# How the first pass of a Fourier-layer kernel stores its chunks: 120 and 8 partitions with 8 KB rows in place of 128 and 128 with 4 KB rows

## The chip, the cores and the metric

The kernel runs on one core of a Trainium2 chip. The metric is the time on the device, in microseconds (us), of one execution; smaller is better. The core has a tensor engine (PE, with its weight loads PEld), a vector engine (DVE), a scalar engine (ACT), GpSimd (POOL) and a sync engine (SP) that here only issues transfers. Sixteen DMA engines carry every transfer between the on-chip memory (SBUF, 128 partitions) and the device memory (HBM).

## What is computed

The reference turns 64 images of 256 x 256 into tokens and runs one transformer layer on them. The front part is a Fourier neural operator of four layers on 32 channels, and it is what the change touches:

```
v = concat([x, gx, gy]) @ p_w + p_b                  # 64 x 32 x 256 x 256
for i in range(4):
    x1 = irfft2(12 x 12 low modes of rfft2(v), mixed over channels by fw1[i], fw2[i])
    x2 = einsum('bcxy,cd->bdxy', v, w_w[i]) + w_b[i]
    v = x1 + x2
    v = (v - mean) * rsqrt(var + eps) * bn_g[i] + bn_b[i]   # mean, var over b, x, y
    if i < 3: v = relu(v)
out = einsum('bcxy,cu->bxyu', v, q_w) + q_b
```

Behind it come a concatenation with 77 text rows, an attention over 333 tokens and a feed-forward block on half of the tokens. All is float32.

## The kernel before, in words

The mean and variance of a layer need all images, so the kernel makes passes. `forward_first` (L215) takes the input's low modes, and `mix` (L428) turns modes into mixed modes and the statistics, once for each of the four layers. Between them stand three passes of `layer` (L546, i = 0, 1, 2), which make the new `v` of layer i and at once what the next layer needs of it. A last stage (`image_rows` L960, `attention` L1054, `feed_forward` L1121) makes the output. `v` is 64 x 8 MB of float32, 512 MB, so it goes through HBM: pass 0 writes it, passes 1 and 2 read the old and write the new, the last stage reads it.

In HBM `v` is one tensor for an image, `[128, 8, 8, S]` (L183): partition, chunk t, row of the chunk, y. A chunk (b, t) is one eighth of an image, 1 MB: 8 rows of 256 numbers on each of 128 partitions, 8 KB a partition that lie together both in SBUF and in HBM; the partitions of one chunk lie 64 KB apart in HBM.

For each chunk `layer` does:

- `pre` (L676): matmuls into four PSUM banks, held as two pairs, from `y_` (the x transform of the mixed modes) and, in pass 0, from `mv` (the y table with four rows of the input x, reloaded for each image by `load_x`, L637, from POOL's queue). In passes 1 and 2 the old `v` comes in instead, through `ld` (L652). `pre` also takes a new `vo` buffer from the pool `lo`, which has 4 (L561, L698).
- `evA` and `evB` (L700): the ReLU of one bank pair into one half of `vo`: evA fills rows 0 to 3, evB rows 4 to 7, each on ACT (L705) or DVE (L707) as the order says.
- `st` (L711): stores `vo` to HBM with two transfers from SP's queue.
- `turn` (L716, DVE transpose L719), `prod` (L724, L730) and `sqA`, `sqB` (L736, L741: squares on ACT for the next statistics) read `vo` too. `y`, `zt`, `half`, `x`, `xo` and `xs` (L745 to L803) make the next layer's modes of an image.

A `vo` buffer is free for the fifth chunk after it when its stores have landed and `turn` and `prod` have read it. PSUM is a ring of four pairs handed out by `take` (L602): a `pre` or a `prod` needs two, and gets those that were closed first.

The order of all this is written out by hand in `ORDER` (L128), one word a step, the first string for pass 0. A suffix `.a` or `.d` names ACT or DVE, `@1` means that the step works on the next image. `layer` runs under a manual schedule, so each engine and each queue takes its instructions in this order. In pass 0 the chunks come in the order 2, 3, 6, 4, 5, 7, 1, 0 (the last two an image ahead), so that chunk 7 takes the buffer of chunk 3, 5 that of 2, 1 that of 6, 0 that of 4, and 2, 3, 6, 4 those of 5, 7, 1, 0 of the image before. SP's queue has, for each image: st1, st2, st0, the two loads of `ams` (mixed modes, L623), st6, st3, st5, st4, st7 and the store `xs`. Chunk 3 is thus stored behind chunk 6.

```
    def st_(b, t, e):
        for n in range(2):
            rows = slice(4 * n, 4 * n + 4)
            nc.sync.dma_start(dst[b][:, t, rows], vo[b, t][:, rows])
```

Of the kernel before, what the change touches and what calls it, by code (L numbers as in the profile page):

```python
# [153 lines left out]
def tile_fno_fusion_transformer(ctx: ExitStack, tc: tile.TileContext, a, cst_d, grid_d, out):  # L154
    nc = tc.nc
# [390 lines left out]
    def layer(i, st, src, dst, acc):  # L546
# [7 lines left out]
        with ExitStack() as cx:  # L554
# [64 lines left out]
            y_, t32, vin, vo, half_, zts = {}, {}, {}, {}, {}, {}  # L619
# [89 lines left out]
                return run  # L709

            def st_(b, t, e):  # L711
                for n in range(2):
                    rows = slice(4 * n, 4 * n + 4)
                    nc.sync.dma_start(dst[b][:, t, rows], vo[b, t][:, rows])
# [87 lines left out]
            def xs(b, n, e):  # L802
                nc.sync.dma_start(xh_d[i][:, b, :], xos.pop(b).rearrange("p g k -> p (g k)"))  # L803

            run = dict(
                am=am, lx=lx, ld=ld, sp=sp, spT=spT, pre=pre, evA=ev(0), evB=ev(1), st=st_, turn=turn,
                prod=prod, sqA=sq(0), sqB=sq(1), y=y, half=half, zt0=zt(0), zt1=zt(1), x=x_, xo=xo, xs=xs,
            )
# [425 lines left out]
```

## Time and profile before

| what | value |
|---|---|
| median of 3 runs | 11274.17 us (11272.87 to 11285.87) |
| the profiled execution's own time | 11293.58 us |
| its span, first to last instruction | 11291.7 us |
| PE, DVE, ACT, POOL busy | 94%, 75%, 57%, 13% of the span |
| DMA packets, bytes | 972,544; 3457.29 MB |
| `v<-vo` (L714), all three passes | 3072 transfers of 512 KB, median 7.8 us from issue to landing |
| the same in pass 0, 300 to 2400 us | least 2.6, median 4.9, most 10.0 us |
| `vin<-v` (L656), passes 1 and 2 | 2048 transfers of 512 KB, 9.1 us |
| `ch<-v` (L980), last stage | 512 transfers of 1024 KB, 12.5 us |

The stages in the span, from the trace: 0 to 200 us the first modes, the first `mix` and the tables; 200 to 2525 pass 0; 2525 to 2667 `mix`; 2667 to 5480 pass 1; 5480 to 5640 `mix`; 5640 to 8500 pass 2; 8500 to 8700 the last `mix` and the weights; from 8700 the transformer.

How to read what follows. Lnnn is a line of the kernel. In a list of waits each line has the engine and line that waited, behind the arrow what ended the wait, then the total in us, the number of times and the longest. In a chain each line has a start, a duration and what was at work, all in us. In a table of stretches each line has the stretch, its length, the busy time of PE, PEld, DVE, ACT and POOL with the number of instructions in brackets, the clock that PE was granted, the mean busy share of the 16 DMA engines and the GB/s that they moved. SPq is SP's queue of issues. The trace also holds a record of every DMA packet with its queue, start, duration and size, but not its engine. It tells when a transfer landed for about a quarter of the stores. Where a busy PE is told, note that matmuls are pipelined and their ends modelled, so waits of less than a microsecond can lie inside busy time.

### The profile page before, as it was taken

The page shows a single profiled execution, that of the slowest core. Times are in us where ns is not written, and L with a number is a line of the kernel's source. Part 1 is how long each engine was busy: PE and PEld are TensorE (multiplying, and loading weights), DVE is VectorE, ACT ScalarE, POOL GpSimd, SP SyncE. Part 2 cuts the span into 40 slices and gives each one's busy share as a digit, 9 for nine tenths or more (in the row PEclk, how much of TensorE's full clock was granted, in tenths as well). Part 3 has the DMA queues.
Part 4 walks back from the last instruction along what each step waited for, and adds up shares of the span by engine and source line. Part 5 has one row for each costly group of instructions (what it writes and reads, how often), then busy time and mean ns, then how long its engine had stood idle before and what let it go on. Part 6 is the DMA issues. An engine that isn't in the chain of part 4 may idle for free.

```text
span 11291.7 us, 409300 instructions
## 1 busy us (share of the span) xinstructions
PE 10625.0 (94%) x182550; PEld 5738.0 (51%) x182550; DVE 8446.5 (75%) x10381; ACT 6473.1 (57%) x10673; POOL 1442.4 (13%) x2179
## 2 busy tenths in 40 slices
PE   6999999998999999999799999999996999999999
PEld 3555555554444444444444444444443666666666
DVE  6888888887777777777677777777775666666665
ACT  5777777775566655566555566655563333333333
POOL 1111111110000000000000000000000333333333
PEclk8999999998999999999899999999998999999999
DMA  6776676678999999999899999999998555555553
GB/s 213 247 250 244 249 247 248 246 253 320 383 376 382 380 377 372 374 379 379 305 375 380 380 376 378 381 380 376 372 379 291 226 227 228 227 227 228 226 227 140
DMA packets 972544, 3457.29 MB, mean 306 GB/s; under 512 B 149784, under 2 KB 199320, under 8 KB 903832
## 3 DMA queue, kind: packets, MB, share of 16 engines
q1 hardware_dynamic: 905344, 3366.80, 77.8%
q0 software_dynamic: 58288, 60.60, 2.3%
q8 instruction: 1428, 23.40, 0.8%
q10 hardware_dynamic: 7144, 3.72, 0.1%
q14 instruction: 340, 2.79, 0.1%
HBM read 1733.60 MB, written 1696.92 MB: 304 GB/s over the span
## 4 chain that ended last, share of the span: by engine, by line
PE 62%; DMA 20%; DVE 9%; ACT 3%; issue 3%; SPq 2%; POOL 0%; ACTq 0%; DVEq 0%; POOLq 0%
PE ring L752 15%; DMA v<-vo 11%; PE ring L682 9%; PE ring L730 8%; DMA vin<-v 6%; PE ring L693 5%; PE hp L982 4%; PE ring L662 3%; PE pp L1145 3%; PE pp L1156 3%; PE ring L786 2%; DVE vo L707 2%; PE pp L1110 2%; PE pp L1175 2%; PE pp L1072 1%
## 5 line engine op out<-in xcount | busy, mean ns | idle before, releaser
L741 ACT ACTIVATE ring<-ring 128x1024 f32<-128x1024 f32 x3072 | 3115.8, 1014 | 1188.4 <-PE ring L730 1119.5
L719 DVE STREAM_TRANSPOSE t<-vo 128x2048 f32<-128x2048 f32 x1536 | 3465.7, 2286 | 20.9 <-DVE vo L707 0.9
L730 PE MATMUL ring<-vo,w 32*32 32x512 f32 x49152 | 2413.1, 600 | 85.0 <-ACT vo L705 68.3
L707 DVE TENSOR_SCALAR vo<-ring 128x1024 f32<-128x1024 f32 x1280 | 1544.5, 1221 | 1199.7 <-PE ring L693 806.6
L705 ACT ACTIVATE vo<-ring 128x1024 f32<-128x1024 f32 x1792 | 1791.7, 1023 | 1044.1 <-PE ring L693 500.9
L752 PE MATMUL ring<-t,cst 32*32 32x512 f32 x49152 | 2072.0, 599 | 51.0 <-issue 44.9
L752 PEld LDWEIGHTS ring<-t,cst 32*32 32x32 f32 x49152 | 913.4, 103 | 925.6 <-issue 622.6
L730 PEld LDWEIGHTS ring<-vo,w 32*32 32x32 f32 x49152 | 803.2, 103 | 1070.2 <-issue 407.1
L693 PE MATMUL ring<-vin,ws 32*32 32x512 f32 x32768 | 1287.8, 603 | 22.9 <-issue 16.2
L682 PE MATMUL ring<-cst,y 24*128 24x256 f32 x16384 | 1230.3, 402 | 77.0 <-DVE vo L707 61.7
L682 PEld LDWEIGHTS ring<-cst,y 24*128 24x128 f32 x16384 | 789.5, 185 | 993.2 <-DVE vo L707 392.4
L631 POOL TENSOR_TENSOR ams<-ams,bns 48x512 f32<-48x512 f32 x384 | 400.5, 1043 | 6989.4 <-DMA ams<-mix 6510.1
L670 DVE STREAM_TRANSPOSE y<-ring 128x1024 f32<-128x1024 f32 x384 | 763.1, 1987 | 329.5 <-PE ring L662 328.5
L682 PE MATMUL ring<-mv,y 29*128 29x256 f32 x8192 | 705.3, 403 | 36.3 <-ACT ring L741 19.6
L682 PEld LDWEIGHTS ring<-mv,y 29*128 29x128 f32 x8192 | 456.9, 185 | 369.0 <-ACT ring L741 209.3
L786 PEld LDWEIGHTS ring<-cst,zt 128*128 128x128 f32 x4608 | 533.6, 193 | 177.1 <-ACT vo L705 114.2
L762 ACT COPY half<-ring 128x1024 f32<-128x1024 f32 x192 | 194.4, 1013 | 731.4 <-PE ring L752 731.4
L1183 POOL DMA_DIRECT2D out_dram<-o x1024 | 508.2, 505 | 659.0 <-DVE o L1178 616.9
L741 ACT ACTIVATION_READ_ACCUMULATOR ring<-ring 128x1 f32 x3072 | 585.6, 191 | 0.0
L786 PE MATMUL ring<-cst,zt 128*128 128x96 f32 x4608 | 565.6, 280 | 6.1 <-DVE zt L770 5.7
L770 DVE STREAM_TRANSPOSE zt<-ring 128x1024 f32<-128x1024 f32 x192 | 377.4, 1965 | 248.1 <-PE ring L752 248.1
L662 PE MATMUL ring<-ams,cst 49*128 49x512 f32 (+1 forms) x1536 | 450.6, 642 | 99.1 <-POOL ams L631 37.2
(374 smaller groups left out, 9762.6 us busy)
## 6 DMA issues: line engine op xcount, KB each, us to landing
v<-vo SPq DMA_DIRECT2D x3072, 512.0 KB, 7.8
vin<-v SPq DMA_DIRECT2D x2048, 512.0 KB, 9.1
ch<-v SPq DMA_DIRECT2D x512, 1024.0 KB, 12.5
mix<-ob SPq DMA_DIRECT2D x96, 512.0 KB, 5.6
ams<-mix SPq DMA_DIRECT2D x384, 96.0 KB, 8.0
xin<-in_x_dram SPq DMA_DIRECT2D x16, 1024.0 KB, 6.5
mv<-in_x_dram POOLq DMA_DIRECT2D x256, 64.0 KB, 7.4
out_dram<-o POOLq DMA_DIRECT2D x1024, 16.0 KB, 3.0
```

Of the source, the lines that this page charges most:

```text
L662: nc.tensor.matmul(ps[:, n, :], lhsT=EX[hv, 128 * h:128 * h + 128], rhs=ams[b % 2][hv], start=True, stop=True, skip_group_check=True,)
L670: nc.vector.transpose(y_[b, h].rearrange("p q c -> p c q"), ring[key][0][1].rearrange("p n (c k) -> p (n c) k", k=32),)
L682: nc.tensor.matmul(ps[n][:, 256 * r:256 * r + 256], lhsT=y_[b, t // 4][32 * n:32 * n + K, q:q + 4, :].rearrange("p q c -> p (q c)"), rhs=m ...
L693: nc.tensor.matmul(ps[n][32 * j:32 * j + 32], lhsT=ws[32 * n:32 * n + 32], rhs=v[32 * n:32 * n + 32, 2 * j:2 * j + 2, :], start=False, sto ...
L705: nc.scalar.activation(to, ring[key][h][1], AF.Relu)
L707: nc.vector.tensor_scalar(to, ring[key][h][1], 0.0, None, ALU.max)
L719: nc.vector.transpose(t32[b, t // 2][:, :, 8 * (t % 2):8 * (t % 2) + 8, :].rearrange("p y s c -> p s y c"), vo[b, t].rearrange("p s (y l) ...
L730: nc.tensor.matmul(ps[n][32 * j:32 * j + 32], lhsT=w4[i + 1][32 * n:32 * n + 32], rhs=vo[b, t][32 * n:32 * n + 32, 2 * j:2 * j + 2, :], st ...
L741: nc.scalar.activation(ps, ps, AF.Square, accum_out=acc[:, at:at + 1])
L752: nc.tensor.matmul(ps[n][32 * j:32 * j + 32], lhsT=FYT[32 * n:32 * n + 32, k, :], rhs=t32[b, j][32 * n:32 * n + 32, k].rearrange("p s c -> ...
L786: nc.tensor.matmul(ps[:, 0, 96 * g:96 * g + 96], lhsT=zt_[:, h, k0:k0 + 4, :].rearrange("p k c -> p (k c)"), rhs=FX[:, h, 48 * r:48 * r + ...
L1183: nc.gpsimd.dma_start(out[b, 64 * n + 16 * g:64 * n + 16 * g + 16].rearrange("(p t) d -> p t d", t=2), o[32 * g + 8 * n:32 * g + 8 * n + 8 ...
```

## The change

In pass 0 (`i == 0`) a chunk is stored by two transfers that split the partitions rather than the rows: partitions 0 to 119 with their whole 8 KB, and partitions 120 to 127 with theirs. The bytes, their places in HBM, the queue, the number of transfers and their place in the order are the same. The first of the two transfers now reads both halves of `vo`. Passes 1 and 2 keep the two transfers of 128 partitions with four rows each.

```diff
             def st_(b, t, e):
+                if i == 0:
+                    for part in (slice(0, 120), slice(120, 128)):
+                        nc.sync.dma_start(dst[b][part, t], vo[b, t][part])
+                    return
                 for n in range(2):
                     rows = slice(4 * n, 4 * n + 4)
                     nc.sync.dma_start(dst[b][:, t, rows], vo[b, t][:, rows])
```

## The prediction, made before the changed kernel was run

> **What bounds the kernel now.** I read the slices of the page first, then the busy times by stage, then the waits inside the first pass, then its chain.
>
> ```profile
> PE   6999999998999999999799999999996999999999
> ...
> DMA  6776676678999999999899999999998555555553
> ```
>
> The digits are tenths of a slice of 282 us. PE is at nine tenths nearly everywhere; the DMA engines are at six or seven tenths in the first pass (slices 2 to 9) and full in the next two. The stages in figures (the last two columns are the DMA share and GB/s):
>
> ```profile
> 200.00:2525.00 2325.00, 2257.05 (x42675) 1181.56 (x42654) 2065.57 (x1148) 1774.20 (x2807) 270.83 (x380) 1.00 0.70 248
> ...
> 2562.90:2564.90 2.00, 1.13 (x71) 1.13 (x74) 1.38 (x5) 1.91 (x3) 0.00 (x0) 1.00 0.73 154
> ...
> 3000.00:3100.00 100.00, 94.65 (x2083) 43.69 (x2087) 76.00 (x42) 58.60 (x94) 6.27 (x6) 1.00 0.99 385
> ```
>
> The first pass lasts 2325 us for 64 images, 36.4 us each, with DMA at 0.70. The two other lines are for later use: with all partitions at work a full DMA carries 385 GB/s, and while `mix` stores 64 partitions (L495) 0.73 of it carries only 154, or 211 when full. The waits from 300 to 2400 us (total, times, longest):
>
> ```profile
> PEld ring L730 <- ACT vo L705: 155.6, 288, 2.1
> ...
> ACT vo L705 <- DMA v<-vo: 26.4, 41, 1.9
> ...
> DVE vo L707 <- DMA v<-vo: 5.1, 7, 0.9
> ```
>
> So the stores do end waits, about once an image, but only 31.5 us in 2100, or 35 us in the whole pass. Where, the chain of one image shows:
>
> ```profile
> 1594.22 1.03 ACT vo L705
> ...
> 1595.70 0.38 SPq L714
> 1596.08 0.05 issue
> 1596.14 0.78 SPq L714
> 1596.91 0.05 issue
> 1596.97 10.13 DMA v<-vo
> ...
> 1607.20 1.03 ACT vo L705
> 1608.23 0.04 issue
> 1608.28 2.06 PE ring L730 x32
> 1610.33 1.73 PE ring L786 x14
> ```
>
> An eviction ends (chunk 6, evA6), SP issues the stores of chunks 6 and 3 together, the last needs 10.13 us to land, and only then may chunk 7 be evicted into chunk 3's buffer; `prod` (L730) and `x` (L786) follow. I matched the instructions with the order written at L128: over 45 images st6 was issued 0.36 and 0.84 us after evA6, st3 1.68 and 3.10 us after it, and the second half of st3 landed at 10.97 (medians). It landed a median of 0.41 us before ev7 began, in the tightest of the 13 images that tell 0.07. For the other buffers this slack is 3.25 us (chunk 4 to chunk 0; least 2.0) or 6.7 and more. One edge is tight, and PE hangs on it at once.
>
> [...] The trace before shows only the 16: an st6 after idle time starts 16 packets within 0.16 us. [...] `mix`'s 64 partitions [...]: its 4 KB packets take 0.32 us, twice 0.16. And the final stage's 16 KB stores of eight partitions (L1183): a 2 KB packet alone takes 0.084 us, eight together 0.08 to 0.21, all done 0.32 us after the first began[...].
>
> **The change part by part.** All of it is in L711 to L714, run 512 times; nothing moves in SP's queue, and there are two issues a chunk as before (0.38 us median).
>
> *Rows of 8 KB.* 65,536 packets fewer. The final stage's 8 KB packets take 0.313 us, twice 4 KB 0.32: under 0.1 us a chunk gained. I count nothing.
>
> *The first store waits for both evictions.* Behind it on SP is only the second store, which waited for the same eviction before; nobody later in the queue is delayed. What is lost is the head start of one half, up to the time between the evictions (st6 is issued at 0.36 and 0.84, so 0.4 us). In the burst of st6 and st3 the engines are full, so the start counts, not the halves: between 0 and 0.4 us; I take 0.1.
>
> *The 120 rows.* [...] 8 x 0.313 = 2.5 us, against 16 x 0.16 = 2.56 before. [...] No run here shows how 120 rows are dealt out. Bounds -0.06 and +2.5 us; I take -0.06 and leave the rest to a rival.
>
> *The 8 rows.* [...] 4 x 0.313 = 1.25 us; at least 0.31 if the engines come one after another. The L1183 stores show the sharing, so I take 1.25.
>
> [...] 2.5 + 1.25 = 3.75 us a chunk against 2.56, +1.2. Share of the pass: 8 x 3.75 = 30 us an image, and other traffic 2.9 us (0.70 less the 0.62 of these stores, of 36.4): 33 of 36.4 us, tight but not over. On the path: st6 and st3 are two chunks in a burst, so st3 lands 2 x 1.2 + 0.1 = 2.5 us later; less the slack of 0.41, ev7 starts 2.1 us later. PE's next work waits for it (L730 behind ACT L705 above), and DVE and ACT behind PE, so I see no cover. The edge from 4 to 0 has st5 and st4 in one burst, +2.4 us against a slack of 3.25 that grows by the delay of ev7: it holds, though fuller queues (the `ams` loads, the `mv` loads of L638[...]) can add 0 to 0.5 us; I take 0.2. Sum: 2.3 us x 64 images = 147 us. [...]
>
> Durations are of the profiled execution: 11,293.6 us, of which the span is 11,291.7 and 1.9 lie around it; this is 0.17% over the median 11,274.2 of the runs. I add the sum to the median: **11,421 us**. Its own range is 11,350 to 11,520: 64 x 1.2 us if the eight rows are half spread, 64 x 3.8 if both edges bind.
>
> **The rivals.**
> *Pairs [...] (slower, more).* For it: `mix`'s packets double [...]. [...] Half in step, a row costs 0.47 us: 8 x 0.47 + 1.25 = 5.0 us a chunk, 40 us an image, with the rest 43, and about one more that the queue can't fill: 44 - 36.4 = 7.6 us, x 64 = 486, **11,760 us**. DMA becomes the bound of the pass. In step throughout: 8 x 6.25 + 2.9 = 53 us an image, 12,340, which I hold for unlikely[...].
> *The stores stay hidden (no change).* The eight rows go out while the engines of the 120 are staggered[...]. Then a burst of two chunks costs 2 x (2.5 + 0.31 - 2.56) = 0.5 us, about the slack of 0.41: 64 x 0.1 = 6 us, **11,280 us**.
> *Faster.* The mechanism: in the burst behind evA6, st3 shares engines with three `mv` loads (L638)[...] and some 4 KB packets there take 1.2 us. [...] its tail shortens by up to 0.6 us. It decides as soon as that exceeds what the eight rows add, at evB7 (L707/L705). The wait it can remove is 35 us in all: **11,240 us**. Against it: pre7 ends only about 0.1 to 0.3 us before ev7 starts, so there is no more to win.
>
> **How the numbers follow.** Chances: forecast 0.38, pairs 0.27, no change 0.21, faster 0.14. About 0.2% (23 us) is what a measurement of this kernel can tell from none. Slower by more: all of the first two and 0.03 of the third, 0.68. Faster by more: 0.10 of the last. Within: 0.22. The range runs from 11,250 (leaving out 0.06 of the faster case) to 11,830 (leaving out about 0.09, the pairs mostly in step).
>
> **What would show it.** In the changed kernel's first pass: ACT's wait for `v<-vo` at the eviction line up from 26 us to some 150; images 38.7 us apart instead of 36.4; DMA packets about 907,000; 8 KB packets of 0.31 us in the large store, and of about 1.2 in the small one. 8 KB packets of 0.6 us throughout, with GB/s in slices 2 to 9 near 200, mean pairs. [...] The other stages must keep their lengths (2813, 2860 and 2591 us). I am wrong if 120 and 8 rows are dealt to all 16 engines by partition[...].

## The result, and the profile after

The changed kernel takes 11,491.3 us (median of 4 runs, 11,479.0 to 11,492.2) beside 11,280.0 for the kernel before (4 runs): ratio 1.0187, 95% interval 1.0175 to 1.0199. That is 211 us more, where 147 were forecast. The profiled execution has a span of 11,489.6 us, 197.9 over the one before. The issue of the last store of the first pass ends at 2724.1 us instead of 2522.5: the pass alone is 201.6 us longer, and the stages behind it keep their lengths.

The slices of the page after the change, PE and DMA in tenths and what the DMA moved in GB/s, then the count of packets:

```profile
PE   6999999997999999999989999999997999999999
...
DMA  6777777777999999999989999999998655555553
GB/s 206 220 228 236 228 226 229 229 231 238 381 384 379 383 376 374 381 381 377 361 325 380 375 381 379 376 375 381 371 375 309 232 231 231 222 221 222 229 230 144
DMA packets 902396, 3457.24 MB, mean 301 GB/s; under 512 B 145176, under 2 KB 194712, under 8 KB 768152
```

PE is again at nine tenths in the first pass, and the DMA engines at seven: busier than before (there sixes and sevens), for fewer bytes a second, yet not full. One stretch of the pass, 300 to 2500 us, in the kernel before and in the changed one (stretch, length, PE, PEld, DVE, ACT, POOL, clock, DMA share, GB/s):

```profile
300.00:2500.00 2200.00, 2138.87 (x40500) 1123.37 (x40498) 1955.52 (x1089) 1678.68 (x2659) 257.60 (x361) 1.00 0.70 248
```

```profile
300.00:2500.00 2200.00, 2021.31 (x37474) 1029.08 (x37473) 1811.65 (x1005) 1555.38 (x2458) 237.18 (x331) 0.98 0.76 229
```

In the same time PE did 37,474 matmuls instead of 40,500. It was busy for 118 us less, and its granted clock fell from 1.00 to 0.98. The waits in this stretch, changed kernel:

```profile
PEld ring L734 <- ACT vo L705: 201.5, 250, 2.9
PEld ring L756 <- issue: 197.8, 389, 5.1
...
PE ring L756 <- issue: 63.7, 38, 4.2
...
ACT vo L705 <- DMA v<-vo: 57.0, 53, 2.3
...
PEld ring L682 <- issue: 48.5, 41, 4.3
...
DVE vo L707 <- DMA v<-vo: 31.6, 34, 2.1
...
PE ring L682 <- issue: 19.9, 12, 3.9
```

The evictions wait for stores for 88.6 us (57.0 + 31.6; 33.3 before). But there is a second group: waits of PE and of its weight loads that end with `issue`, that is, with nothing that the profile shows. Before, the same three lines read:

```profile
PEld ring L752 <- issue: 116.2, 430, 1.6
...
PEld ring L682 <- issue: 5.1, 7, 0.8
PE ring L752 <- issue: 2.1, 6, 0.7
```

(L752 then is L756 now.) The wait of the matmuls themselves at this line went from 2.1 us to 63.7, and its longest from 0.7 to 4.2 us. On the chain of waits such a stop stands beside a late store (parts of one image, left-out lines marked):

```profile
1553.13 1.23 ACT ring L745 x3
1554.36 2.61 issue
1556.97 1.20 PE ring L682 x16
...
1567.91 1.95 ACT vo L705 x2
...
1570.63 1.06 SPq L714
1571.70 0.04 issue
1571.74 9.74 DMA v<-vo
```

**What ends these stops.** The page has a queue named instruction, q8, with the same line in this kernel and in the one before (packets, MB, share of the engines):

```profile
q8 instruction: 1428, 23.40, 0.8%
```

That is 16 KB a packet, and 64 bytes for each of PE's 365,100 matmuls and weight loads (23.40 MB over 365,100): I read it as the fetch of PE's program. In the first pass one comes about every 7 us (318 from 300 to 2500 us before, 294 after). I call a stretch of over 1 us in which neither a matmul nor a weight load runs a stop, and a *fetch stop* if it ends 1.1 to 1.8 us after the end of a q8 packet (chance would give one in ten). From 300 to 2500 us the kernel before has none; the changed one has 55 stops, 99.2 us, of which 36 are fetch stops, 74.5 us. The fetches themselves are not slower (median 949 ns, before 967): they start late.

That PE lacked instructions can be checked without the times. 16 KB are 256 instructions of 64 bytes. If PE's 365,769 records (365,100 and the sequencer's) are numbered in order, all 36 fetch stops lie behind a record with the same remainder modulo 256, namely 193. Of the other 19 stops one does. So PE stops where a block ends. The same count gives how many records PE had left when each fetch started: in none of the 14 traces more than 303, thus little more than one block. Fewer than 60 were left in 11 of 318 fetches before (never under 34), and in 61 of 294 in the changed kernel, 23 of them with none.

The clock is slower too: it stood at 0.5 for 68.3 us in 16 pieces (before: never), and 13 of the 16 begin from 0.5 us ahead of the end of a stop of 1.5 us or more to 2 us behind it. At half speed 68.3 us lose 34.

So an image takes 39.55 us on average instead of 36.46 (images 4 to 63). In the 2200 us, PE and its loads idle together for 3.19 us an image instead of 0.99, which is +2.20, of which the fetch stops are 1.34 (74.5 us over 55.6 images); the slow clock is 34 us over as many, +0.61; 0.28 of the 3.09 us remain unassigned.

### The profile page after: what moved, and what is told of

Its sections match the earlier page's. It is cut to its first block, busy times and chain, and to the rows that moved or that the text cites. A ratio compares the mean times of both kernels' runs of the same rounds, so it can differ in the third digit from the quotient of the medians.

```text
span 11489.6 us, 408919 instructions
## 1 busy us (share of the span) xinstructions
PE 10677.8 (93%) x182550; PEld 5732.2 (50%) x182550; DVE 8451.8 (74%) x10381; ACT 6472.9 (56%) x10673; POOL 1442.2 (13%) x2179
## 2 busy tenths in 40 slices
DMA packets 902396, 3457.24 MB, mean 301 GB/s; under 512 B 145176, under 2 KB 194712, under 8 KB 768152
## 3 DMA queue, kind: packets, MB, share of 16 engines
q8 instruction: 1428, 23.40, 0.8%
## 4 chain that ended last, share of the span: by engine, by line
PE 52%; DMA 20%; DVE 7%; ACT 3%; issue 3%; SPq 2%; POOL 0%; ACTq 0%; POOLq 0%; DVEq 0%
DMA v<-vo 13%; PE ring L756 12%; PE ring L682 6%; DMA vin<-v 6%; PE ring L734 6%; PE ring L693 5%; PE hp L986 3%; PE ring L662 3%; PE pp L1149 3%; PE pp L1160 3%; PE pp L1114 2%; DVE vo L707 2%; PE ring L790 2%; PE pp L1179 2%; ACT vo L705 2%
## 5 line engine op out<-in xcount | busy, mean ns | idle before, releaser
L756 PE MATMUL ring<-t,cst 32*32 32x512 f32 x49152 | 2103.4, 603 | 127.6 <-issue 113.5
L756 PEld LDWEIGHTS ring<-t,cst 32*32 32x32 f32 x49152 | 905.5, 103 | 1037.1 <-issue 724.4
```

Source lines behind the costliest of these rows:

```text
L756: nc.tensor.matmul(ps[n][32 * j:32 * j + 32], lhsT=FYT[32 * n:32 * n + 32, k, :], rhs=t32[b, j][32 * n:32 * n + 32, k].rearrange("p s c -> ...
```

## The experiments

Theory A was the prediction's: rows read at the same time slow each other, the rows 120 to 127 and pairs of the 120, so stores land late and an eviction waits for its buffer. Theory C came from the trace: PE's fetches wait behind the stores' packets. Before the runs I took the length of the packets to be what matters in C. That didn't hold for one transfer a chunk (e6), and D took its place: a fetch waits for all that was queued on its engine before it.

A *pile* is two chunks whose stores SP issues back to back: 2 and 0, 6 and 3, 5 and 4. The expectations of e1, e2 and e4 speak of 126 stops, or about a hundred, of over 1.5 us; that is an earlier count of the changed kernel, and in the way defined above it has 29. Diffs are against the changed kernel. The figures behind the time are from 300 to 2500 us, all in us except the number of fetch stops; the time of e8 holds zeros that are written besides:

| run | us over before | waits for the stores | fetch stops | slow clock |
|---|---|---|---|---|
| before | 0 | 33.3 | 0 | 0 |
| changed | 211 | 88.6 | 36, 74.5 us | 68.3 |
| e1 one transfer, 8 KB | 75 | 1.5 | 24, 38.2 us | 23.9 |
| e2 split, four transfers, 4 KB | 49 | 66.6 | 1, 1.0 us | 0 |
| e3 one transfer and eight rows more | 128 | 4.2 | 27, 62.1 us | 112.6 |
| e4 chunk 3 before 6 | 202 | 88.9 | 43, 78.5 us | 71.7 |
| e5 split, two transfers, 4 KB | 167 | 142.6 | 12, 20.4 us | 47.8 |
| e6 one transfer, 4 KB | 67 | 16.2 | 18, 24.7 us | 6.8 |
| e7 chunk 4 before 5 | 168 | 29.5 | 37, 69.8 us | 61.4 |
| e8 120 rows alone | (405) | 112.5 | 54, 125.9 us | 180.9 |
| e9 one transfer, 8 KB, two queues | -4 | 3.6 | 1, 1.8 us | 0 |
| e10 changed, two queues | 107 | 70.1 | 10, 13.9 us | 20.5 |
| e11 as e9, issued closer | 11 | 0 | 5, 6.0 us | 0 |
| e12 before, two queues | -2 | 1.4 | 3, 4.5 us | 3.4 |

### e1: one transfer of 128 partitions

```diff
-                    for part in (slice(0, 120), slice(120, 128)):
-                        nc.sync.dma_start(dst[b][part, t], vo[b, t][part])
+                    nc.sync.dma_start(dst[b][:, t], vo[b, t])
```

> Each chunk of the first pass goes out as one transfer of 128 partitions with 8 KB rows: the long rows and the wait for both evictions of the change, without its partition split. Theory A (late landing: [...] the store of chunk 3 lands late and eviction 7 waits): [...] 8 KB packets of 0.31 us and 11,280 us, give or take 15. Theory C (PE's instruction fetch waits behind long packets, whatever makes them long), in the form that 8 KB alone is long enough: PE still has about a hundred stops of over 1.5 us with no releaser, 11,350 to 11,450 us. In the form that only packets of 0.6 us and more do it: 11,280 us, and a handful of such stops.

11,356.9 us, ratio 1.0060 (1.0048 to 1.0073). The packets take 314 ns (median), twice the 160 of the 4 KB packets before, so they are not slowed, and nobody waits long for a store: in the waits only this is left of them.

```profile
ACT vo L705 <- DMA v<-vo: 1.5, 4, 0.5
```

Still it loses 75 us, and all 24 of its stops are fetch stops. By the count of blocks, too, all 24 lie where a block ends. Here A is excluded, so this is the case in which to look at one of them. Its stretch in the timeline (start, duration, engine, line; in brackets the idle time ahead and what ended it):

```profile
512.07 0.79 SPq L713 DMA_DIRECT2D v<-vo  x2
...
518.92 0.48 PE L682 MATMUL ring<-mv,y 29*128 29x256 f32 x1
520.83 1.14 PE L682 MATMUL ring<-mv,y 29*128 29x256 f32 x15 [1.43 <-issue]
```

SP issues the stores of chunks 2 and 0 back to back. What the DMA did then, as busy times by stretch (a packet counts in full where it starts, so a share can exceed 1):

```profile
516.00:517.00 1.00, 1.00 (x50) 0.65 (x34) 1.00 (x1) 0.08 (x1) 0.00 (x0) 1.00 1.04 401
...
519.40:520.80 1.40, 0.00 (x1) 0.00 (x0) 0.34 (x1) 0.00 (x0) 0.00 (x0) 1.00 0.05 15
```

and the packets by queue from 513.4 to 518.4 us, then from 518.4 to 519.6 us:

```profile
q1 hardware_dynamic: 257, 1.85, 98.4%
```

```profile
q1 hardware_dynamic: 118, 0.17, 41.2%
q8 instruction: 1, 0.02, 4.9%
```

For five microseconds the engines carry the two stores and no fetch. The fetch starts at 518.5 us, as they run dry, and takes 0.95 us; PE has used up its instructions at 519.40 and goes on at 520.83. During the stop the DMA is nearly idle (0.05). In 19 of the 24 stops the fetch starts over 5 us after the last issue, when both chunks of the pile are through; in the others 2.6 to 3.4 us after it. 18 of the stops follow the pile of chunks 2 and 0, six that of 6 and 3, and none that of 5 and 4, which SP issues just as close. A fetch may be as late there, but PE needs it later: in the 6 us after the first issue PE starts 357 records behind chunk 2, 259 behind 6 and 172 behind 5.

### e2: the split with twice as many transfers

```diff
+                    for n in range(2):
+                        rows = slice(4 * n, 4 * n + 4)
                     for part in (slice(0, 120), slice(120, 128)):
-                        nc.sync.dma_start(dst[b][part, t], vo[b, t][part])
+                        nc.sync.dma_start(dst[b][part, t, rows], vo[b, t][part, rows])
```

> The partition split of the change (0 to 119, 120 to 127), but each transfer cut in halves of 4 KB rows as before the change: four transfers a chunk. Theory A: [...] the stores take as many bytes' time: 11,450 to 11,550 us, the upper end because SP issues twice as many transfers (0.4 us each). Theory C by size of packet: a fetch waits behind packets half as long, PE's stops of over 1.5 us fall from 126 to under 40, and the time to 11,330 to 11,420 us. If C goes by the bytes queued ahead and not by the packet, the stops stay at about 126 and the time is as under A.

11,331.8 us, 1.0039 (1.0024 to 1.0054): in the interval that C by size of packet had given. The packets are slowed as in the changed kernel (a tenth of them takes 347 ns or more, against 182 in the kernel before), the DMA share is larger than in the changed kernel, 0.80, and the fetch stops are gone (the one of the table doesn't lie at the end of a block). What is left is the wait for stores, 66.6 us, nearly all ahead of the eviction of chunk 7 (57.7). So the split of the partitions with small transfers, and with twice the issues on SP, costs 49 us. Packets and transfers are both half as long here; e5 and e6 part them.

### e3: eight rows more

```diff
+    extra = [dram.tile([8, 8, 8, S], F32, name=f"extra{b}") for b in range(B)]
...
-                    for part in (slice(0, 120), slice(120, 128)):
-                        nc.sync.dma_start(dst[b][part, t], vo[b, t][part])
+                    nc.sync.dma_start(dst[b][:, t], vo[b, t])
+                    nc.sync.dma_start(extra[b][:, t], vo[b, t][120:128])
```

> One transfer of 128 partitions with 8 KB rows, and after it a second one of partitions 120 to 127 into a scratch array that nothing reads (extra work; the result isn't changed). It measures the eight rows by themselves. Theory A as predicted: they take 1.25 us a chunk [...], of which two chunks lie ahead of eviction 7: 11,400 to 11,430 us. Rival (the cost is in the 120 rows read in pairs): 11,280 to 11,320 us, and ACT's wait for v<-vo stays under 45 us from 300 to 2600 us. Theory C: [...] few stops of PE, below 20 of over 1.5 us.

11,410.8 us, 1.0112 (1.0098 to 1.0126): in the interval that A gave, and not by A's way. Beside e1 the eight rows cost 54 us, while the evictions wait 4.2 us for stores in all; fetch stops grow from 38.2 to 62.1 us (69.1 by the count of blocks), and the slow clock from 23.9 to 112.6 us. Only 8 of the 18 drops of the clock begin that near to the end of a stop of 1.5 us or more here, so they are not explained by the stops alone. The time fitted; only the trace tells that the cause was another.

### e4 and e7: another order of two stores

```diff
-   st6 ... st3          (e4)        -   st5 ... st4          (e7)
+   st3 ... st6                      +   st4 ... st5
```

> The changed kernel with the stores of chunks 3 and 6 in exchanged places in SP's order (chunk 3 was ready long before): chunk 3 then lands one chunk earlier, 3 to 4 us, and eviction 7 has no store to wait for. Theory A: the whole loss was this edge, 11,270 to 11,310 us. Theory C: PE's stops without a releaser don't hang on it; they stay at about 126 of over 1.5 us, and at most the 63 us by which the waits for v<-vo had grown are won back: 11,420 to 11,490 us.

11,484.1 us, 1.0178 (1.0164 to 1.0192), no gain that can be told. Matching the waits with the order tells why: in the changed kernel only 13.5 us of them stand ahead of chunk 7, and 71.7 ahead of chunk 0, which takes chunk 4's buffer. With e4 the first are gone, and those ahead of chunk 0 are 83.4.

> The changed kernel with the stores of chunks 4 and 5 in exchanged places in SP's order. In the changed kernel 72 us of the 89 us of waits for v<-vo (300 to 2500 us) stand ahead of the eviction of chunk 0, which reuses chunk 4's buffer. Theory A in its second form (this edge is late, not that of eviction 7): 11,410 to 11,440 us. Theory C alone (the waits only fill time that the fetch stops cost anyway): 11,470 to 11,500 us.

11,455.5 us, 1.0145 (1.0130 to 1.0161). Here the waits for stores fall from 88.6 to 29.5 us, under those of the kernel before:

```profile
ACT vo L705 <- DMA v<-vo: 28.7, 28, 1.7
...
DVE vo L707 <- DMA v<-vo: 0.8, 2, 0.5
```

That wins 43 of 211 us (211 - 168), give or take some 20 by the intervals, and lies between the two expectations, in neither. The 37 stops that remain are all fetch stops. Late landing at this edge is a part of the loss, but the smaller one.

### e5 and e6: the same transfers with packets of 4 KB

```diff
+    vh = [dram.tile([128, 2, 8, 4, S], F32, name=f"vh{b}") for b in range(B)]
...
-                        nc.sync.dma_start(dst[b][part, t], vo[b, t][part])
+                        nc.sync.dma_start(vh[b][part, :, t], vo[b, t][part].rearrange("p (n r) y -> p n r y", n=2))
```

(e6 has one transfer with all partitions in the place of two; pass 1 reads `vh[b][:, n, t]`.)

> The two transfers a chunk of the changed kernel (partitions 0 to 119 and 120 to 127, [...] same waits, same number of issues), but into a DRAM array laid out so that each partition's 8 KB lies in two places: the packets are 4 KB. The second pass reads that array in the same 4 KB rows as before. Theory C (PE's instruction fetch queues behind long packets): the stops of PE of over 1 us near the end of a fetch vanish (36 in the changed kernel from 300 to 2500 us, under 5 here), the granted clock stays at 1.00, and 11,290 to 11,340 us. Theory A [...]: 11,450 to 11,500 us.

> One transfer of 128 partitions a chunk, but with 4 KB packets, into the same split array. Beside the run with 8 KB packets (11,357 us) only the length of the packets differs. Theory C: 11,250 to 11,285 us, no stop of PE of over 1 us near a fetch (24 there). If the 75 us there came from the single transfer (no head start of one half, one issue less), it stays at 11,340 to 11,370.

Both miss what C gave. e6 takes 11,354.4 us, 1.0058 (1.0045 to 1.0070), as much as e1 with packets twice as long and where the alternative put it, and has 18 fetch stops. e5 takes 11,454.3 us, 1.0152 (1.0138 to 1.0166), in A's interval. In e5 the fetch stops did fall, from 36 to 12, but the waits for stores rose, now mostly ahead of chunk 7 (91.5 us):

```profile
ACT vo L706 <- DMA vh<-vo: 121.4, 86, 4.2
...
DVE vo L708 <- DMA vh<-vo: 21.2, 24, 2.0
```

So with one transfer a chunk the length of a packet is not the cause. With the split it is less clear: e5 has 54 us less of fetch stops than the changed kernel and is only 44 us faster, with 54 us more of waits for stores, and which of the two the split causes by itself was not parted. What e1 and e6 have in common, and the kernel before has not, is one transfer of 1 MB instead of two of 512 KB. By estimate that is 2.6 us instead of 1.3: in the kernel before, the first 16 packets of a store on idle engines start within 0.15 us (median), and 16 at a time make 16 rounds of 0.160 us of the 256 packets in 1 MB (with 8 KB, 8 of 0.314). To see this directly I counted when fetches start: per 100 us in which fewer than 12 packets of stores were in flight (the quiet time), and per 100 us in a burst, by the time since 12 or more had been in flight (300 to 2500 us; entries move by some units, the last column's by more, with how a burst is delimited; that the first two kernels lie above the other three from 1 to 4 us doesn't):

```
kernel        quiet   1 to 4 us into a burst   where they crowd: rate at us into the burst
before        17.5    13.1                     32 at 1.5-2.0, 27 at 4.0-4.5, 61 at 5.5-6.0
e2            15.0    19.2                     30 at 2.0-2.5, 52 at 3.0-3.5
e1            21.0     6.3                     13 at 2.5-3.0, 44 at 5.5-6.0
e6            22.1     8.4                     18 at 2.5-3.0, 40 at 5.5-6.0
changed       20.5     5.5                     32 at 4.5-5.0, 35 at 7.0-7.5
```

In the kernel before, fetches slip in behind the first transfer (1.3 us), with e1 and e6 behind the first of 2.6 us or only behind both. So a fetch starts mostly where a transfer ends, and often waits for two of them (19 of 24 stops in e1). Why it gets in there, no run shows.

### e8: the 120 rows alone

```diff
-                    for part in (slice(0, 120), slice(120, 128)):
-                        nc.sync.dma_start(dst[b][part, t], vo[b, t][part])
+                    nc.sync.dma_start(dst[b][0:120, t], vo[b, t][0:120])
```

> Only the transfer of partitions 0 to 119 is left; what belongs to partitions 120 to 127 of the first pass isn't stored, and zeros that are written ahead of the pass stand in its place (33.5 MB, estimated at 90 us of DMA), so the output isn't the reference's, and the pass is judged by the period of its images (36.5 us before, 37.7 with one transfer of 128 rows of 8 KB, 38.8 with eight extra rows, 39.6 in the changed kernel). If the rows 0 to 119 in pairs cause most: 38.5 to 39.5 us and packets of 600 to 650 ns as often as in the changed kernel. If the eight rows cause it: 37.5 to 37.9 us.

The 33.5 MB at the 385 GB/s of 3000 to 3100 us in the kernel before are 87 us.

An image takes 41.4 us, more than in the changed kernel, though a sixteenth of the bytes is left out: under neither expectation. A tenth of the packets takes 645 ns or more, exactly as in the changed kernel, so the slow packets come from the 120 rows and not from the eight. The fetch stops are the most of all runs (54, 125.9 us, all at the end of a block), and the waits for stores, 112.5 us, are more than in the changed kernel too. Here, as in e1, SP's issue of chunk 3 ends only 0.45 us after that of chunk 6; in the changed kernel the small transfer lies between and it is 1.5 us (medians). A closer pile fits D, but that this is why it is worse was not tried by itself.

### e9, e10, e11: the pile taken apart

```diff
-                        nc.sync.dma_start(dst[b][part, t], vo[b, t][part])
+                        (nc.scalar if t in (0, 3) else nc.sync).dma_start(dst[b][part, t], vo[b, t][part])
...
-   ... sqB0 st0 ... sqA4 st3 sqB4 ...
+   ... sqA3 st3 ... sqA7 st0@1
```

(This is e10; e9 is the same edit on e1.)

> One transfer of 128 partitions with 8 KB rows a chunk, as in the run that took 11,357 us, but chunks 0 and 3 are issued from ACT's queue, 3 us and more away from the stores of chunks 2 and 6, with which SP issued them 0.5 us apart. Size of packet and of transfer are the same; only the pile of two chunks is gone. Theory D (a fetch of PE waits for the stores that were queued on its engine before it, so the harm is in the pile of 5.1 us): the stops of PE of over 1 us near a fetch fall from 24 to under 5, and 11,260 to 11,300 us; an issue costs ACT something that no run has shown, an estimate of 0.4 us each as on SP. If it is the size of a single transfer (2.6 us): the stops stay at 15 to 30 and the time at 11,330 to 11,370 us.

> The changed kernel (120 and 8 partitions, 8 KB rows) with the same move: chunks 0 and 3 issued from ACT's queue, away from chunks 2 and 6. Theory D: half of the piles are gone (chunks 5 and 4 still go together), PE's stops near a fetch fall from 36 to 5 to 15, eviction 7 and 0 wait as in the changed kernel or less: 11,350 to 11,420 us. [...] 11,450 to 11,500 us.

Both fall where D put them (the other interval of e10 is A's). e9 takes 11,282.1 us, 0.9998 (0.9989 to 1.0006): with the same packets and the same transfers as e1 the whole 75 us are gone, and with them all stops but one. Fewer than 60 records were left to PE in 3 of 318 fetches, in e1 in 39 of 308. The three `issue` lines of PE and its loads shown above are back near the kernel before:

```profile
PEld ring L755 <- issue: 118.8, 435, 2.7
...
PEld ring L682 <- issue: 8.4, 10, 1.1
...
PE ring L755 <- issue: 3.1, 5, 1.8
```

e10 takes 11,392.9 us, 1.0096 (1.0082 to 1.0110): 104 us less than the changed kernel's 211, fetch stops down from 74.5 to 13.9 us; the waits for stores stay (70.1 us).

Two things changed at once in e9, though: the distance (chunk 3 is issued 2.2 us after 6; chunk 0 is issued 5.5 us ahead of 2, and 1.5 us after 1) and the queue. The pile of 5 and 4 stayed, 0.43 us apart on SP's queue, and did no more harm than in e1. Within a burst the fetches of e9 are nearly as rare as those of e1: 7 to 9 per 100 us from 1 to 4 us into it, depending on how a burst is delimited, in e1 5 to 6, in the kernel before 12 to 13. So its transfers hold fetches up as well. But behind chunk 2, where e1 has 18 of its 24 stops, no second chunk is queued any more. This speaks for the distance and doesn't prove it. e11 was to put the two close together again on two queues:

> As the run with one transfer of 128 partitions and chunks 0 and 3 on ACT's queue (11,282 us), but these two are now issued right after the evictions A2 and A6, within about half a microsecond of chunks 2 and 6 on SP's queue: two queues as there, the pile of two chunks as in the run with SP alone (11,357 us). Theory D in its plain form (what counts is how much is queued on an engine at once, on whatever queue): stops of PE of over 1 us near a fetch return, 15 to 30 from 300 to 2500 us, and 11,330 to 11,370 us. If a fetch waits only for a pile within one queue, so that the second queue was the cure: under 5 stops, 11,265 to 11,300 us.

11,295.7 us, 1.0011 (1.0003 to 1.0019), 5 fetch stops (6 by the count of blocks, 5 of them behind chunks 0 and 2). But it did not make the pile: ACT's queue issued its stores before the eviction ahead of them in program order had ended, 1.7 and 1.5 us before SP's. That is closer than in e9 and not as close as the 0.4 us of e1, and the stops lie between as well. Whether the second queue or the distance is the cure stays open.

### e12: the kernel before with two queues

> The kernel before the change (two transfers of 128 partitions with 4 KB rows a chunk), with chunks 0 and 3 issued from ACT's queue, away from chunks 2 and 6. It had no stop of over 1 us near a fetch to lose, but 33 us of waits for v<-vo from 300 to 2500 us, ahead of evictions 6, 7 and 5. If the move takes these away as it did with one transfer a chunk (to under 5 us): 11,245 to 11,270 us; if something else, such as the issues on ACT (0.33 us each), takes their place: 11,275 to 11,300 us.

The edit is that of e10 with the kernel's old halves of rows. 11,282.6 us, 0.9996 (0.9988 to 1.0005): no difference. The waits for stores went from 33.3 to 1.4 us, and 3 fetch stops (4.5 us) came in; an image takes 36.46 us in both. No version tried is faster than the kernel before.

## Why the prediction was right, and where it was wrong

The direction was right, and so was the time: 11,350 to 11,520 contains it, and the value is 70 us low. The way there was mostly another, so that the number came out so near is in large part luck: one cost that was put at nothing took the place of others that were put too high.

*Rows of 8 KB: "I count nothing".* This is the step that failed first. The price of a row was right (0.316 us measured, median), but the DMA engines also bring PE its instructions (q8, 16 KB about every 7 us), and the change queues 960 KB in one transfer where 512 KB stood, and with the next chunk twice that. By itself (e1) this costs 75 us. e6 loses as much with rows of 4 KB, so it isn't the row; e9 shows that it goes when the piles are taken apart over two queues. I had seen only the stores' own readers in the waits; the fetch queue stood on the page with 0.8%, and the prediction has no term for it.

*The first store waits for both evictions, 0.1 us.* Nothing in the runs speaks against it: e9, with one store that waits for both, is as fast as the kernel before. The engines were full in the burst of chunks 6 and 3, as the prediction took them to be: DMA share 0.92 to 1.11 in each microsecond from 1596 to 1600 of the trace before.

*The 120 rows: -0.06 us, the rest left to a rival.* The eight rows at 0.313 us one after another were an estimate. The trace after bears out their number, 120 rows over 15: in 70 of the 77 stores that start on idle engines 15 packets are in flight 0.9 us after the start, in the other 7 14. But the rival had a point. Where a store so starts, 13 of its second fifteen packets take 595 to 650 ns and one 305 to 325 (in order of start, medians over the 77), as seven pairs that slow each other and a single one would. Of the third fifteen all take 595 to 650, of the fifth 9 take 305 to 325: the packets are slow at the start and part of them fast after some four rows. The trace doesn't name the engines, so what a pair shares isn't shown. In the pass the 8 KB packets have a median of 316 ns, a mean of 429 and a tenth above 645, so the truth lies between the forecast and "half in step". But the DMA did not become the bound, as that rival said (share 0.76, 229 GB/s).

*The 8 rows: 1.25 us a chunk.* The factor four was an estimate from the last stage's stores of eight partitions: in the trace before, a 2 KB packet alone takes 0.084 us, and 495 groups of eight are done 0.34 us (median) after their first began. e3 prices them at 54 us in all beside e1, where 2 x 1.2 x 64 = 154 us were counted on the path; in the changed kernel packets of about 1.2 us are hardly to be seen (99 of 100 take at most 0.914 us), in e3 there are some (1,707 of 61,803 take over 1.1 us, in e1 60 of 59,894). And what they cost in e3 isn't a wait for stores; fetch stops and the slow clock grew instead.

*The path: eviction 7.* Wrong edge. It waits 13.5 us for stores, and taking these away (e4) brings nothing; the edge from 4 to 0, which I let hold with a slack of 3.25 us, waits 71.7 us. There SP issues chunk 4's two transfers at 12.97 and 14.86 us after evA6 instead of 10.15 and 11.38, which I hadn't counted. The two issues themselves last 1.7 and 1.9 us there instead of 0.41 and 1.12; no run shows the reason. e7 gives the worth of this edge, 43 us.

*The signs.* ACT's wait for `v<-vo` was to reach 150 us and reached 57.0, with DVE 88.6. Images were to be 38.7 us apart: the mean is 39.55, the median 38.4. Packets: 907,000 against 902,396; I had left out the 4,608 small ones (149,784 to 145,176 under 512 B). The GB/s are at 220 to 238, not at 200.

How much of the 211 us each part has can be told roughly: 75 for the large transfer alone (e1) and 43 for late landing (e7). The rest of about 90 has no experiment of its own: fetch stops and the slow clock grow when the same bytes also go in 120 and 8 partitions (74.5 and 68.3 us beside 38.2 and 23.9), but e5 has few fetch stops and loses 167 us all the same. The parts overlap (e10 wins 104 us from two of the three piles), so these aren't a sum.

## What to carry to other kernels

When transfers are merged or lengthened, ask who else is served by the same DMA engines, the program's own fetch above all: with PE at nine tenths and a fetch every 7 us, a pile of 5 us of stores on one queue stopped it (24 times in 2200 us of e1). Ask also how fast the program runs through its instructions just then: the pile of chunks 5 and 4 was as close and did no harm. Look for waits that end with nothing (`issue`), and lay them beside the packets of the instruction queue. And a time that fits is not a mechanism: e3 hit its number while the waits that were to cause it weren't there.

## What the runs showed of the hardware that was not expected

- PE's fetches, 16 KB each (q8: 23.40 MB in 1428 packets), were held up by stores for 5 us and more: in e1 none ran from 513.4 to 518.4 us, and in 19 of its 24 stops the fetch started over 5 us after the last issue. They got in mainly where a transfer ended (e1: 44 per 100 us at 5.5 to 6.0 us into a burst, 6.3 from 1 to 4 us). In the changed kernel this cost 74.5 us in 2200. In no trace did PE have more than 303 instructions left when a fetch started, little more than one block of 256, and a block lasts about 7 us; so a fetch that comes about that late stops it.
- In the changed kernel 13 of the 16 drops of PE's granted clock to 0.5 come with one of its 29 stops of 1.5 us or more. 13 of the 16 drops last 3.4 us, the others 6.8 or 10.2 us. At half speed 3.4 us lose 1.7 beyond the stop itself. In e3 only 8 of 18 drops come so, and what else brings them isn't shown.
- In a store of 120 partitions that starts on idle engines 15 packets are in flight at once (70 of 77 stores, 0.9 us after the start). 13 of the second and all of the third fifteen take 595 to 650 ns for 8 KB, 9 of the fifth 305 to 325; with 128 partitions (e1) the median is 314.
- ACT's queue issues a store before the end of the eviction that precedes it in the program: in e11 the issue of chunk 0's store ends 0.8 us before evA2 does (10.42 and 9.65 us ahead of the end of evA6).
